# Weighting the experts' rows in their tiles and adding them in DRAM, instead of reading them back and combining them

## The chip, the cores and the metric

The kernel runs on one core of one Trainium2 chip. The metric is the device time of one execution in microseconds. Three timed runs of the kernel before took 3605.23, 3607.03 and 3609.01 us; the median is 3607.03 us.

## The reference, cut to what matters

The program is two layers, each a graph attention network and a feed-forward part, on 4096 rows of 256 floats, with a residual sum after every part. The change lies wholly in the last part, a mixture of six experts with the best two chosen for each row:

```python
def _L1_ffn_ref(features, router_w1, ..., expert_b3):      # E, TOP_K = 6, 2
    rh = relu(features @ router_w1 + router_b1)
    expert_logits = softmax(rh @ router_w2 + router_b2)
    top_w, top_i = top_k(expert_logits, TOP_K)
    routing_weights = softmax(top_w)
    h1 = relu(einsum('bsd,edh->bseh', features, expert_w1) + expert_b1)
    h2 = relu(einsum('bseh,ehf->bsef', h1, expert_w2) + expert_b2)
    expert_out = einsum('bsef,efo->bseo', h2, expert_w3) + expert_b3
    sel = take_along_axis(expert_out, top_i[:, :, :, None], axis=2)
    return sum(sel * routing_weights[..., None], axis=2)

x = x + _L1_ffn_ref(layernorm(x)[None], ...)[0]
```

All of it is in 32-bit floats. The kernel computes an expert only for the rows that chose it.

## The kernel before, in words

The program is written with a framework that sets semaphores by itself and orders the instructions of each engine by its own scheduler, so the order on an engine is not always that of the source. In the source, `P` is 128, `C` is 256, `G` is 4, so a group is 512 rows and there are `NG` = 8 groups; `T` is 2 · 4096 / 256 + 5 = 37 tiles of `TR` = 256 rows.

The first three parts (attention, a feed-forward of 30 steps, two more attention layers) end at about 3240 us of the profiled span. The last part has four stages.

*Router* (L808 to L853). For each group of 512 rows the kernel loads the rows from `x3d` (L92), takes the layer norm on DVE (L100, L833), writes the normed rows `n` to the DRAM tensor `nd` (L836), turns them with PE (L113), copies them to SBUF (`fT`, L838, ACT), and multiplies by the router's weights (L822, L845). The hidden layer `rh` is made by ACT (L824). ACT also writes the rows less 1 to the SBUF tile `acc` (L839), which holds all 4096 rows; the residual stream carries a 1 too much, hence the 1. While this goes on, SP's queue brings in the experts' weights (L857).

*List* (L860 to L1036). DVE picks the two best experts of each row, counts the rows of each expert and lays the 8192 pairs of row and choice into 37 tiles, each tile of one expert. Places that stay empty are padded. The results are `source`, the row that a place reads from `nd`; `dest`, the row of the DRAM tensor `yd` that it writes; and `ws`, the two weights of each row. In `yd` each pair of row and choice has a row of its own: row `n` for the first choice, 4096 + `n` for the second, and rows after that for the padding.

*Tiles* (L1038 to L1146). For each tile, POOL gathers two times 128 rows from `nd` into `gx` (L1048, four buffers); PE turns them (L1060), DVE copies them (`xT`, L1062); PE computes two hidden layers (L1083) and the result (L1104), with weights that DVE and ACT copy for the tile's expert (L1076); ACT (L1094) and DVE (L1096) add bias and take the ReLU. DVE adds the last bias (`ye`, L1112, three buffers) and POOL scatters the 256 rows to `yd`, in two transfers of 128 rows (L1114). The scatters are declared independent of one another:

```python
for before_ in scatters:
    tc.declare_no_dep(ins.ins, before_, reason="a permutation: ...")
scatters.append(ins.ins)
```

In the source, iteration `i` issues the gather of tile `i + 2`, the first hidden layer of tile `i`, the result and scatter of tile `i − 1`, the turning of tile `i + 1` and the second hidden layer of tile `i`.

*End* (L1147 to L1163). After the last scatter SP's queue loads, group by group, both choices' rows from `yd` (16 loads of 512 KB, L1149). DVE multiplies each by its weight and adds it to `acc` (64 operations, L1160), and ACT's queue writes the group to the output (8 writes of 512 KB, L1163).

Of the kernel before, what the change touches and what calls it, by code (L numbers as in the profile page):

```python
# [44 lines left out]
def gnn_ffn_kernel(ctx: ExitStack, tc: tile.TileContext, a: dict, out: bass.AP):  # L45
# [732 lines left out]
    with ExitStack() as scope:  # L778
# [2 lines left out]
        T2 = 2 * T  # L781
        one = scope.enter_context(tc.tile_pool(name="m_one", bufs=1))
        bT = one.tile([P, NB], F32, name="bT")
        acc = one.tile([P, NT, C], F32, name="acc")
        ws = one.tile([P, 2, NT], F32, name="ws")
        bsel = one.tile([P, T, 2 * KC], F32, name="bsel")
        expert = one.tile([P, T], I32, name="expert")
        dest = one.tile([P, T2], I32, name="dest")
        source = one.tile([P, T2], I32, name="source")
        ew = [one.tile([P, E, KC, C], F32, name=f"ew{i}") for i in range(3)]  # L790
        b3 = one.tile([P, E, C], F32, name="b3")
        nd = dram.tile([N, C], F32, name="nd")
        yd = dram.tile([2 * N + T * TR, C], F32, name="yd")

        with ExitStack() as rs:
            work = rs.enter_context(tc.tile_pool(name="r_work", bufs=2))
# [7 lines left out]
            ps = bank("ps_s")  # L804
            nc.tensor.transpose(ps[:, :NB], br, ident[:NB, :NB])
            nc.vector.tensor_copy(bT, ps[:, :NB])

            lg = rone.tile([P, NT, E], F32, name="lg")  # L808
            rows, stds, fTs, rhs = {}, {}, {}, {}
# [2 lines left out]
            for g in range(NG + 2):  # L812
                if 1 <= g and g + 2 < NG and g + 2 not in ahead:
                    load_ahead(x3d, g + 2, runs_of)
                if g < NG:
                    rows[g] = ahead.pop(g)
                    stds[g] = over_std(work, rows[g])
                if 2 <= g:
                    ps = bank("ps_r")
                    fT = fTs.pop(g - 2)  # L820
                    for k in range(KC):
                        nc.tensor.matmul(ps[:RH], rw1[:, k, :], fT[:, k, :], start=(k == 0), stop=(k == KC - 1))  # L822
                    rh = rhs[g - 2] = work.tile([RH, GR], F32, name="rh")
                    nc.scalar.activation(rh, ps[:RH], AF.Relu, bias=bT[:RH, 0:1])  # L824
                if 1 <= g <= NG:
                    u = g - 1
                    t = rows.pop(u)
                    rstd, mv = stds.pop(u)
                    nmr = work.tile([P, G], F32, name="nmr")
                    nc.vector.scalar_tensor_tensor(nmr, mv[:, :, 0], -1.0, rstd, op0=OP.mult, op1=OP.mult)  # L830
                    n = work.tile([P, G, C], F32, name="n")
                    for r in range(G):
                        nc.vector.tensor_scalar(  # L833
                            n[:, r, :], t[:, r, :], rstd[:, r : r + 1], nmr[:, r : r + 1], op0=OP.mult, op1=OP.add
                        )
                    nc.sync.dma_start(runs_of(nd, u), n)  # L836
                    fT = fTs[u] = work.tile([P, KC, GR], F32, name="fT")
                    nc.scalar.copy(fT, transposed(ps_t, n))  # L838
                    nc.scalar.activation(acc[:, u * G : (u + 1) * G, :], t, AF.Identity, bias=mone)  # L839
                if 2 <= g:  # L840
                    u = g - 2
                    rh = rhs.pop(u)
                    ps = bank("ps_l")
                    for r in range(G):
                        nc.tensor.matmul(  # L845
                            ps[:, r * E : (r + 1) * E], rh[:, r * P : (r + 1) * P], rw2, start=True, stop=True
                        )
                    nc.vector.tensor_tensor(
                        lg[:, u * G : (u + 1) * G, :],
                        ps[:, : G * E].rearrange("p (r e) -> p r e", e=E),  # L850
                        rb2[:, None, :].to_broadcast([P, G, E]),
                        OP.add,
                    )  # L853
# [14 lines left out]
            HB = NT // 2  # L868
            along = numbers("along", [(1, max(T, N // TR))], 0, 0)
            along16 = numbers("along16", [(1, P), (0, HB)], 0, 0, F16)  # L870
            place = numbers("place", [(P, T2)], 2 * N + GR, 1)


            code = rone.tile([P, 2, NT, 2], F16, name="code")
# [36 lines left out]
            for i in range(2):  # L911
                tops.append(best(lg, f"top{i}"))
                oh = hot[:, i]
                nc.vector.tensor_tensor(oh, lg, over(tops[i]), OP.is_equal)
                nc.vector.tensor_tensor(oh, oh, order, OP.mult)
                nc.vector.tensor_tensor(oh, oh, over(best(oh, f"at{i}")), OP.is_equal)
                if i == 0:
                    nc.vector.scalar_tensor_tensor(lg, oh, -4.0, lg, op0=OP.mult, op1=OP.add)

# [77 lines left out]
            df = rone.tile([P, T2], F32, name="df")  # L999
            nc.vector.scalar_tensor_tensor(df, lst[:, :, 1], float(GR), lst[:, :, 0], op0=OP.mult, op1=OP.add)  # L1000
            nc.vector.scalar_tensor_tensor(df, df, -float(GR), none, op0=OP.add, op1=OP.add)
            sf = rone.tile([P, T2], F32, name="sf")
            nc.vector.tensor_scalar(sf, df, float(N), -float(N), op0=OP.is_ge, op1=OP.mult)
            nc.vector.tensor_tensor(sf, sf, df, OP.add)
            nc.vector.tensor_scalar(source, sf, float(N - 1), None, op0=OP.min)
            nc.vector.tensor_copy(dest, df)

            seen = rone.tile([P, T, E - 1], F32, name="seen")
            nc.vector.tensor_tensor(
# [17 lines left out]
                OP.mult,  # L1027
            )
            nc.vector.tensor_reduce(bsel, sel, axis=AX.X, op=OP.add)

            w1, w2 = ws[:, 0], ws[:, 1]
            nc.vector.tensor_tensor(w2, tops[1], tops[0], OP.subtract)
            nc.scalar.activation(w2, w2, AF.Exp)
            nc.vector.tensor_scalar(w1, w2, 1.0, None, op0=OP.add)
            nc.vector.reciprocal(w1, w1)
            nc.vector.tensor_tensor(w2, w2, w1, OP.mult)  # L1036

        work = scope.enter_context(tc.tile_pool(name="m_work", bufs=3))  # L1038
        ps_t = scope.enter_context(tc.tile_pool(name="m_pst", bufs=2, space=PSUM))
        ps_h = scope.enter_context(tc.tile_pool(name="m_psh", bufs=2, space=PSUM))  # L1040
        ps_o = scope.enter_context(tc.tile_pool(name="m_pso", bufs=2, space=PSUM))
        rows, xT, hT, which, held = {}, {}, {}, {}, {}
        scatters = []

        def gather(i):
            rows[i] = work.tile([P, 2, C], F32, name="gx", bufs=4)
            for r in range(2):
                nc.gpsimd.indirect_dma_start(  # L1048
                    out=rows[i][:, r, :],
                    out_offset=None,  # L1050
                    in_=nd[:, :],
                    in_offset=bass.IndirectOffsetOnAxis(ap=source[:, 2 * i + r : 2 * i + r + 1], axis=0),
                )

        def turn(i):
            src = rows.pop(i)
            pt = ps_t.tile([P, KC, TR], F32, name="pt")
            for k in range(KC):
                for r in range(2):
                    nc.tensor.transpose(pt[:, k, r * P : (r + 1) * P], src[:, r, k * P : (k + 1) * P], ident)  # L1060
            xT[i] = work.tile([P, KC, TR], F32, name="xT")
            nc.vector.tensor_copy(xT[i], pt)  # L1062

# [34 lines left out]
        def result(i):  # L1098
# [11 lines left out]
                    )  # L1110
            y = work.tile([P, 2, C], F32, name="ye")
            nc.vector.tensor_tensor(y, po, b3[:, bass.DynSlice(which[i], 1)].to_broadcast([P, 2, C]), OP.add)  # L1112
            for r in range(2):
                ins = nc.gpsimd.indirect_dma_start(  # L1114
                    out=yd[:, :],
                    out_offset=bass.IndirectOffsetOnAxis(ap=dest[:, 2 * i + r : 2 * i + r + 1], axis=0),
                    in_=y[:, r, :],
                    in_offset=None,
                )
                for before_ in scatters:  # L1120
                    tc.declare_no_dep(
                        ins.ins, before_, reason="a permutation: no two of the list's places have one row of yd"
                    )
                scatters.append(ins.ins)

        gather(0)
# [1 line left out]
        for i in range(T + 1):  # L1128
# [15 lines left out]
            if i < T:  # L1144
                hidden(i, 1, h)
                last_h = hT.pop(i)  # L1146
        def back(g, i):  # L1147
            y = work.tile([P, G, C], F32, name="y", bufs=8)
            nc.sync.dma_start(y, runs_of(yd, i * NG + g))  # L1149
            return y  # L1150

        ys = {}
        for g in range(NG + 3):
            if g < NG:
                ys[g] = [back(g, i) for i in range(2)]
            if 3 <= g:
                for i, y in enumerate(ys.pop(g - 3)):
                    for r in range(G):
                        t = (g - 3) * G + r
                        nc.vector.scalar_tensor_tensor(  # L1160
                            acc[:, t, :], y[:, r, :], ws[:, i, t : t + 1], acc[:, t, :], op0=OP.mult, op1=OP.add
                        )
                nc.scalar.dma_start(runs_of(out, g - 3), acc[:, (g - 3) * G : (g - 2) * G, :])  # L1163


# [28 lines left out]
```

## Time and profile before

| what | us |
|---|---|
| median of three runs (lowest to highest) | 3607.03 (3605.23 to 3609.01) |
| the profiled execution | 3589.64 |
| its span, from first to last instruction | 3587.7 |
| router stage, about | 3238 to 3292 |
| list, about | 3292 to 3327 |
| tiles, first gather to last scatter's start | 3327.7 to 3548.4 |
| end | 3548.4 to 3587.7 |

The profile is of one execution. Its engines are PE (matrix products), PEld (PE's weight loads), DVE, ACT and POOL; SP only issues transfers. A line of the timeline gives start, duration, engine, line of the kernel, operation and, in brackets, the idle time of the engine before it and what ended that. Releasers are inferred from semaphore events: where the engine named had long been done, it was another one. A table by stretches gives the busy time of each engine in each, the clock granted to PE, the share of time in which the DMA engines were busy, and what they moved in GB/s. A line on a DMA queue gives packets, megabytes, and the share of the 16 DMA engines' time.

The granted clock of the whole execution was 0.963. On POOL, the 74 gathers have a median of 962 ns each and land 2.8 us after their start; the 74 scatters have 986 ns and land after 2.4 us.

### The profile page before, as it was taken

How to read it: one execution, taken by the hardware profiler on the slowest of the kernel's cores; microseconds unless marked ns; L12 is line 12 of the kernel's file. 1: busy time of each engine (PE TensorE's matmuls, PEld its weight loads, DVE VectorE, ACT ScalarE, POOL GpSimd, SP SyncE). 2: the span in 40 equal slices, each digit the busy share in tenths (PEclk: the TensorE clock that was granted, in tenths of full speed). 3: DMA queues.
4: the chain of work that ended last, by engine and by line, in shares of the span. 5: the costliest groups of instructions: out<-in, count | busy, mean ns of one | idle time of the engine just before them, and what ended most of it. 6: DMA issues, size and time to landing. Idle time of an engine off the chain costs nothing. (4 is left out here: it accounts for less than half of the span.)

```text
span 3587.7 us, 81089 instructions
## 1 busy us (share of the span) xinstructions
PE 3264.7 (91%) x33523; PEld 2981.2 (83%) x33523; DVE 3002.9 (84%) x6039; ACT 2615.2 (73%) x2902; POOL 1100.6 (31%) x899
## 2 busy tenths in 40 slices
PE   6889999996999999999998899999979999996895
PEld 5779889885888888888886889888878888884784
DVE  6899999997877777877786899999889999997445
ACT  2688888886766666666663999999789999993221
POOL 3211101005877777777761000000000000001662
PEclk8899999998999999999998999999999999997897
DMA  6897887501000000000015031321212231314224
GB/s 136 145 232 141 192 196 135 168 22 55 1 1 1 1 1 1 1 1 1 1 31 194 17 119 33 125 75 66 85 66 78 89 123 44 119 25 135 83 95 182
DMA packets 280202, 288.48 MB, mean 80 GB/s; under 512 B 97149, under 2 KB 230426, under 8 KB 279834
## 3 DMA queue, kind: packets, MB, share of 16 engines
q1 hardware_dynamic: 198770, 224.18, 19.2%
q0 software_dynamic: 73920, 52.97, 9.7%
q10 hardware_dynamic: 7144, 6.16, 0.6%
q8 instruction: 264, 4.33, 0.5%
q14 instruction: 104, 0.85, 0.1%
HBM read 248.01 MB, written 68.81 MB: 88 GB/s over the span
## 5 line engine op out<-in xcount | busy, mean ns | idle before, releaser
L565 PE MATMUL acc<-vals,m 128*128 128x130 f16 (+1 forms) x24576 | 1726.6, 232 | 128.2 <-DVE u L475 89.0
L565 PEld LDWEIGHTS <-m 128*128 128x128 bf16 x24576 | 1625.2, 98 | 215.6 <-issue 95.5
L464 ACT ACTIVATE st<-f1b,f2b 128x1024 bf16<-128x1024 f32 (+2 forms) x1664 | 1660.2, 1071 | 152.6 <-DVE m L533 144.8
L533 DVE TENSOR_TENSOR m<-st,m 128x2048 bf16<-128x2048 bf16 (+2 forms) x832 | 938.1, 1137 | 37.0 <-PE acc L565 28.4
L708 PE MATMUL po<-wT,zT 128*128 128x256 f32 x3840 | 875.1, 381 | 10.3 <-ACT zT L734 10.1
L708 PEld LDWEIGHTS po<-wT,zT 128*128 128x128 f32 x3840 | 715.8, 192 | 99.8 <-ACT zT L734 12.4
L694 POOL TENSOR_TENSOR th<-th,y 128x1024 f32<-128x1024 f32 x240 | 567.8, 2367 | 196.2 <-ACT th L693 195.4
L538 DVE TENSOR_TENSOR m<-m,m 128x2048 bf16<-128x2048 bf16 (+2 forms) x520 | 592.8, 1140 | 25.1 <-PE tp_m L217 0.5
L105 POOL TENSOR_TENSOR ln_rstd<-ln_rstd,mhalf 128x4 f32<-128x4 f32 x272 | 281.7, 1036 | 904.1 <-DVE ln_rstd L104 877.3
L100 DVE BATCH_NORM_STATS2 ln_st<-z 128x6 f32<-128x256 f32 x960 | 337.9, 413 | 191.3 <-ACT z L699 191.3
L734 ACT COPY zT<-tp 128x1024 f32<-128x1024 f32 x240 | 242.8, 1012 | 323.7 <-PE tp L113 323.7
L718 DVE SCALAR_TENSOR_TENSOR y<-po,ln_rstd,bias 128x256 f32<-128x256 f32 x928 | 378.6, 469 | 5.2 <-PE po L708 4.4
L699 ACT ACTIVATE z<-th 128x1024 f32<-128x1024 f32 x240 | 254.5, 1060 | 18.5 <-POOL th L694 18.2
L113 PE MATMUL tp<-ident,z 128*128 128x128 f32 x1920 | 251.2, 274 | 12.3 <-ACT z L699 12.3
L113 PEld LDWEIGHTS tp<-ident,z 128*128 128x128 f32 x1920 | 225.9, 142 | 38.9 <-ACT z L699 15.3
L693 ACT ACTIVATE th<-y 128x1024 f32<-128x1024 f32 x240 | 251.2, 1047 | 4.8 <-DVE y L718 4.7
L207 POOL DMA_DIRECT2D rows<-in_adj_dram x80 | 72.9, 912 | 490.6 <-PE tp_m L217 490.3
L447 POOL MEMSET hs<- 128x4 f32 x3 | 0.3, 101 | 630.5 <-DVE u L488 609.1
L305 PE MATMUL ph<-g_w,xT 128*128 128x264 f32 x384 | 112.6, 454 | 30.9 <-DVE v L375 27.7
L305 PEld LDWEIGHTS ph<-g_w,xT 128*128 128x128 f32 x384 | 84.5, 227 | 50.8 <-issue 16.6
L1076 ACT COPY w<-ew 128x512 f32 x37 | 22.7, 617 | 132.8 <-PE ph L1083 103.5
L475 DVE TENSOR_TENSOR u<-acc,lo 128x520 f32<-128x520 f32 (+1 forms) x104 | 66.6, 654 | 49.0 <-ACT lo L474 48.8
(209 smaller groups left out, 2141.6 us busy)
## 6 DMA issues: line engine op xcount, KB each, us to landing
m<-edges SPq DMA_DIRECT2D x32, 2048.0 KB
rows<-in_adj_dram POOLq DMA_DIRECT2D x64, 448.0 KB, 8.0
edges<-ms SPq DMA_DIRECT2D x64, 448.0 KB
m<-edges SPq DMA_DIRECT2D x16, 1792.0 KB
f1b<-fd SPq DMA_DIRECT2D x32, 512.0 KB
rows<-x1d SPq DMA_DIRECT2D x16, 512.0 KB
y<-yd SPq DMA_DIRECT2D x16, 512.0 KB
f1b<-fd SPq DMA_DIRECT2D x16, 448.0 KB
```

What stands on the lines that cost most here:

```text
L100: nc.vector.bn_stats(st[:, r, :], src[:, r, :])
L105: nc.gpsimd.tensor_tensor(rstd, rstd, mhalf, OP.pow)
L113: nc.tensor.transpose(ps[:, k, r * P : (r + 1) * P], src[:, r, k * P : (k + 1) * P], ident)
L464: nc.scalar.activation(st[:, s, :w], f1b[c, h][:, :w], AF.Relu, bias=f2b[:, 2 * q + s, h : h + 1], scale=BIG)
L533: nc.vector.tensor_tensor(m1[:, :, :w], st[:, :, :w], m, OP.logical_and if turned(q) else OP.min)
L538: nc.vector.tensor_tensor(m2[:, :, :w], m, m1[:, :, :w], OP.subtract)
L565: nc.tensor.matmul(acc[:, i, cols], lhs[:, s, rows], v[:, cols], start=(j == 0 and n_ == 0), stop=(j == NT - 1 and n_ == 1), skip_group_ch ...
L693: nc.scalar.activation(th[at], y[:, g * G : (g + 1) * G, :], AF.Tanh, scale=0.01)
L694: nc.gpsimd.tensor_tensor(th[at], th[at], y[:, g * G : (g + 1) * G, :], OP.add)
L699: nc.scalar.activation(z, th.pop(at - 1), AF.Silu, scale=0.01)
L708: nc.tensor.matmul(po[:, r, :], src[:, k, r * P : (r + 1) * P], wT[:, k, :], start=(k == 0), stop=(k == KC - 1),)
L718: nc.vector.scalar_tensor_tensor(y[:, g * G + r, :], po[:, r, :], rstd[:, r : r + 1], last if end else bias, op0=OP.mult, op1=OP.add,)
```

## The change

The experts' results are multiplied by their weights inside the tile loop and are added to the residual rows in DRAM.

- In the router stage ACT's residual rows go to a two-buffer tile `x3` and from there to rows 0 to 4095 of `yd`. `yd` shrinks to 4096 + 256 rows; the last 256, for the padding, are filled with zeros.
- `nd` gets two more columns. The weights of both choices are worked out earlier in the list stage and written into these columns, 8 bytes for each row, by eight transfers on SP. The writes of the normed rows become pieces of 1 KB with a step of 1032 bytes.
- `dest` loses the distinction of the choices (4096 is taken away for a second choice), and padding places of all tiles share the same 256 rows. `which2` keeps which of the two choices a place belongs to.
- In a tile, the gather brings 258 columns; DVE picks the weight of the place (`both`, `weight`), ACT multiplies the two halves of the result by it, and the scatter is a transfer that adds to what `yd` holds.
- Only the two scatters of one tile are still declared independent; a scatter now depends on those of the tile before it.
- At the end there are eight copies from `yd` to the output, DRAM to DRAM, in turn on SP's and ACT's queues. `acc`, the loads and the 64 DVE operations are gone.

```diff
-        acc = one.tile([P, NT, C], F32, name="acc")
-        ws = one.tile([P, 2, NT], F32, name="ws")
+        which2 = one.tile([P, 2, T2], F32, name="which2")
-        nd = dram.tile([N, C], F32, name="nd")
-        yd = dram.tile([2 * N + T * TR, C], F32, name="yd")
+        nd = dram.tile([N, C + 2], F32, name="nd")
+        yd = dram.tile([N + TR, C], F32, name="yd")
...
+            nothing = rone.tile([P, 2, C], F32, name="nothing")
+            nc.gpsimd.memset(nothing, 0.0)
+            nc.sync.dma_start(yd[N:, :].rearrange("(p r) c -> p r c", r=2), nothing)
...
-                    nc.sync.dma_start(runs_of(nd, u), n)
+                    nc.sync.dma_start(runs_of(nd, u)[:, :, :C], n)
...
-                    nc.scalar.activation(acc[:, u * G : (u + 1) * G, :], t, AF.Identity, bias=mone)
+                    x3 = work.tile([P, G, C], F32, name="x3")
+                    nc.scalar.activation(x3, t, AF.Identity, bias=mone)
+                    nc.sync.dma_start(runs_of(yd, u), x3)
...
-            place = numbers("place", [(P, T2)], 2 * N + GR, 1)
+            place = numbers("place", [(0, T), (P, 2)], 2 * N + GR, 1)
...
+            ws = rone.tile([P, NT, 2], F32, name="ws")
+            w1, w2 = ws[:, :, 0], ws[:, :, 1]
+            nc.vector.tensor_tensor(w2, tops[1], tops[0], OP.subtract)
+            nc.scalar.activation(w2, w2, AF.Exp)
+            nc.vector.tensor_scalar(w1, w2, 1.0, None, op0=OP.add)
+            nc.vector.reciprocal(w1, w1)
+            nc.vector.tensor_tensor(w2, w2, w1, OP.mult)
+            for g in range(NG):
+                nc.sync.dma_start(runs_of(nd, g)[:, :, C:], ws[:, g * G : (g + 1) * G, :])
...
-            sf = rone.tile([P, T2], F32, name="sf")
-            nc.vector.tensor_scalar(sf, df, float(N), -float(N), op0=OP.is_ge, op1=OP.mult)
-            nc.vector.tensor_tensor(sf, sf, df, OP.add)
-            nc.vector.tensor_scalar(source, sf, float(N - 1), None, op0=OP.min)
+            nc.vector.tensor_scalar(which2[:, 1], df, float(N), None, op0=OP.is_ge)
+            nc.vector.scalar_tensor_tensor(df, which2[:, 1], -float(N), df, op0=OP.mult, op1=OP.add)
+            nc.vector.tensor_scalar(source, df, float(N - 1), None, op0=OP.min)
             nc.vector.tensor_copy(dest, df)
+            nc.vector.tensor_scalar(which2[:, 0], which2[:, 1], -1.0, 1.0, op0=OP.mult, op1=OP.add)
...
-        scatters = []
...
-            rows[i] = work.tile([P, 2, C], F32, name="gx", bufs=4)
+            rows[i] = work.tile([P, 2, C + 2], F32, name="gx", bufs=4)
...
+            both = work.tile([P, 2, 2], F32, name="both")
+            nc.vector.tensor_tensor(
+                both, src[:, :, C:].rearrange("p r s -> p s r"), which2[:, :, 2 * i : 2 * i + 2], OP.mult
+            )
+            weight[i] = work.tile([P, 2], F32, name="weight", bufs=4)
+            nc.vector.tensor_tensor(weight[i], both[:, 0], both[:, 1], OP.add)
...
+            w = weight.pop(i)
+            scatters = []
             for r in range(2):
+                nc.scalar.activation(y[:, r, :], y[:, r, :], AF.Copy, scale=w[:, r : r + 1])
                 ins = nc.gpsimd.indirect_dma_start(
                     out=yd[:, :],
                     out_offset=bass.IndirectOffsetOnAxis(ap=dest[:, 2 * i + r : 2 * i + r + 1], axis=0),
                     in_=y[:, r, :],
                     in_offset=None,
+                    compute_op=OP.add,
                 )
                 for before_ in scatters:
-                    tc.declare_no_dep(ins.ins, before_, reason="a permutation: ...")
+                    tc.declare_no_dep(ins.ins, before_, reason="no row is twice among an expert's")
                 scatters.append(ins.ins)
...
-        (back: 16 loads of yd, 64 weighted additions to acc, 8 writes to the output)
+        for g in range(NG):
+            (nc.sync, nc.scalar)[g % 2].dma_start(runs_of(out, g), runs_of(yd, g))
```

## The prediction

> **What bounds the kernel now.** The chain of waits puts the end of the program in the mixture-of-experts part; everything up to about 3240 us is attention and feed-forward code that the diff does not touch. So I cut the last 350 us into stages first (busy time of each engine by stretch):
>
> ```profile
> core 0: us, PE busy (x) PEld busy (x) DVE busy (x) ACT busy (x) POOL busy (x), PEclk, DMA share, GB/s
> 3238.00:3292.00 54.00, 41.63 (x223) 27.18 (x221) 32.47 (x132) 23.41 (x27) 15.89 (x30) 0.84 0.64 213
> 3292.00:3327.00 35.00, 9.55 (x68) 8.49 (x68) 30.70 (x64) 0.69 (x3) 0.00 (x0) 0.56 0.05 18
> 3346.00:3518.00 172.00, 172.00 (x857) 151.85 (x857) 83.51 (x154) 44.75 (x92) 120.75 (x123) 1.00 0.30 94
> 3549.00:3588.00 39.00, 0.00 (x0) 0.00 (x0) 26.22 (x64) 0.00 (x0) 0.34 (x1) 0.50 0.84 326
> ```
>
> Four stages with four limits: the router (PE and latency), the list making (DVE, DMA idle at 0.05), the loop over 37 tiles (PE busy 172.00 of 172.00), and a tail of 39 us in which DMA runs at 0.84 and PE not at all. Next, one period of the loop in the timeline, POOL and then PE's weight loads:
>
> ```profile
> 3402.03 0.96 POOL L1048 DMA_INDIRECT gx<-nd,source  x1 [0.77 <-PE pt L1060]
> 3403.30 1.00 POOL L1114 DMA_INDIRECT yd<-ye,dest  x1 [0.30 <-issue]
> 3404.60 0.99 POOL L1114 DMA_INDIRECT yd<-ye,dest  x1 [0.30 <-issue]
> 3405.89 0.99 POOL L1048 DMA_INDIRECT gx<-nd,source  x1 [0.30 <-issue]
> 3407.65 0.96 POOL L1048 DMA_INDIRECT gx<-nd,source  x1 [0.77 <-PE pt L1060]
> ```
> ```profile
> 3403.11 1.70 PEld L1083 LDWEIGHTS ph<-xT,w 128*128 128x128 f32 x8
> 3404.83 1.70 PEld L1104 LDWEIGHTS po<-ew,h 128*128 128x128 f32 x8
> 3406.56 0.57 PEld L1060 LDWEIGHTS pt<-ident,gx 128*128 128x128 f32 x4
> 3407.10 1.60 PEld L1083 LDWEIGHTS ph<-h,w 128*128 128x128 f32 x8
> ```
>
> The period is 3407.65 − 3402.03 = 5.62 us. PE's loads abut: 1.70 + 1.70 + 0.57 + 1.60 = 5.57, so **PE sets the pace**. POOL is second: four transfers of 0.96 to 1.00 plus three gaps of 0.30 and one of 0.77. Only the 0.77 exceeds the usual 0.30, so POOL has 0.47 us of slack per tile. One answer of the waits misleads:
>
> ```profile
> DVE ye L1112 <- DMA yd<-ye,dest: 33.7, 29, 1.2
> ```
>
> It says results wait for scatters. But the ye at 3401.35 is the eleventh (first 3345.16, 5.62 apart) and its buffer, one of three, was scattered at 3386 to 3388, landing by 3391. It was released by PE; the scatter of 3398.98 only happens to land then (2.4 us later). No scatter holds the loop. Last, the tail:
>
> ```profile
> 3548.38 0.97 POOL L1114 DMA_INDIRECT yd<-ye,dest  x1 [0.30 <-issue]
> 3550.92 21.91 SPq L1149 DMA_DIRECT2D y<-yd  x16
> 3557.83 26.38 ACTq L1163 DMA_DIRECT2D out_dram<-acc  x8
> q1 hardware_dynamic: 2304, 8.39, 61.2%
> q10 hardware_dynamic: 1152, 4.19, 28.5%
> ```
>
> From the last scatter's start to the end of the span are 3587.7 − 3548.4 = 39.3 us. In them 8.39 MB come back and 4.19 MB go out, at 350 GB/s: bound by DMA.
>
> **What the Trainium skill says.** All from "DMA: Bandwidth & Descriptors". "Rules for kernel authors": an accumulating transfer reads its destination and writes it later, so an earlier one to the same bytes must be waited for by its semaphore; no run here shows it, since before there is no such transfer. "Two DMAs through the same engine are not ordered": two read-modify-writes issued back to back overlap, the second reading before the first has written; I conclude that the rows of one transfer are pipelined. "Latency and other measured facts": copies from HBM to HBM reached 207 to 214 GB/s in each direction. The trace has no such copy; with one side in SBUF it shows 350 GB/s. The price of an accumulation stands on no page.
>
> **Part by part.** *Tail.* Removed: 16 loads and 64 DVE operations of L1160. Added: 8 copies of 512 KB on SP and ACT, 4.19 MB. At 214 GB/s (the skill's figure, my estimate) that is 19.6 us. Two bounds: 4.19 MB at the 381 GB/s that q1 shows (8.39 MB in 61.2% of 36 us) is 11 us; at 175, if the 4 KB pieces cost more, 24. Around it: landing of the last scatter 3.5 (below), 0.1 to issue, 1.0 to first bytes (SP issues at 3550.92, DMA is busy from about 3551.9), 1.0 for the last receipt (2.4 landing − 0.97 issue − 0.41 transfer). Sum 25.2; gain 39.3 − 25.2 = 14.1, ends 9 and 23.
>
> *Loop, compute.* DVE gets two 128x4 and 128x2 operations per tile, about 0.15 each (nmr L830 is 0.152); ACT gets two scalings of 128x256, 0.84 together (as the pair of L1094). DVE is at 84 of 172 us, ACT at 45: both stay hidden behind PE. The gather now also waits for the DVE product that reads its last two columns; ye ends at 3402.04, the product at about 3402.2, so the gather starts 0.3 to 0.4 later. Queued behind it are the two scatters and the next gather; all slide by the same 0.4 once, since POOL's 5.13 still fits in 5.62. Gathers run six tiles ahead of the scatters in POOL's order (14 before the first scatter), so PE does not see it. Rows of 1032 instead of 1024 B: hidden, DMA share is 0.30. At the last tile nothing covers the scaling: +0.5.
>
> *Loop, the new wait.* A scatter of tile i may start only when both of tile i−1 have landed. Behind the waiting instruction stand a scatter and two gathers; PE would wait for those gathers. The loop through POOL is: start of the first to start of the second scatter 1.30, landing L, waking 0.30. It binds if 1.30 + L + 0.30 > 5.62, that is **L > 4.0**. A plain scatter lands in 2.4, a gather in 2.8. An adding one reads HBM like a gather and writes HBM like a scatter: at most their sum less the shared 0.97 of issue, 4.2; at least 2.4. I take 3.5: hidden by the two gathers issued between. This is only an estimate: the adder itself could cost more.
>
> *POOL's issue cost.* An adding descriptor has two sources. L207 issues 448 KB, 896 rows, in 0.91 us, as long as 128 indirect rows, so rows are not what POOL pays for. I take 1.05; ends 0.97 and 1.5. Slack 0.47 over two scatters: it binds from 1.22.
>
> *Router.* acc (L839) becomes a two-buffer tile with a write of 512 KB per group: 4.19 MB, plus 0.26 MB of zeros, are added to the 11.5 MB of 54 us (213 GB/s), making 295 GB/s, below the 350 seen. Row loads queued behind on SP come up to 8 us ahead of use (issued 3254.12, used 3262 and later). L839, 1.15 us, no longer runs early (four of them by 3252) but within each group's 4.35 us; in the worst order it stands ahead of rh: 1.15 × 6 = 7. I take +2.0, ends 0 and 8. The weights: 4096 pieces of 8 B in nd, behind the expert weights on the rings. 256 B pieces took 17.7 ns each (2080 in 6.4% of 16 × 36 us); at that price 4.5 us over 16 engines, at four times that 18. They are known at 3298.6 and the first gather starts at 3327.7: cover 29 us, at nothing; if the expert weights end 15 us later that cover is gone, and the 8 above includes it. Moved weight formulas sit among the top-two operations already in the trace (3297.2 to 3298.6): nothing. The list gets as many DVE operations before source as before: nothing.
>
> **Sum:** −14.1 + 0.5 + 2.0 = −11.6. The profiled execution took 3589.64 us (span 3587.7 and 1.9 around it), so 3578.0 there; the runs' median is 17.4 higher, 3607.0, and the same difference gives **3595.4**.
>
> **Rivals.** *A, the additions pace the loop* (slower). L = 5 makes the period 1.30 + 5 + 0.30 = 6.60, 0.98 more in 36 steps = +35; with −11.6 that is +24, 3631. It eats the gain from L = 4.3 and is measurably slower from L = 4.5. For it: nothing here prices the adder. Against: the 4.2 bound, and pipelined rows. POOL paying 1.5 per issue (+0.55 × 37 = +20) would look alike but leave no waits.
>
> *B, no change.* The copy at 175 GB/s (gain 9), and the router at +5: −4, 3603. For it: router groups are tight and SP carries 17 more transfers; against: DMA idles at 0.05 after.
>
> *C, the copy runs at the rate of plain transfers:* gain 23 − 2.5 = 20, 3587. In the name of the change nothing else is promised that could fail to be done.
>
> **How the numbers follow.** Expected case, C included, 0.58; A 0.27; B 0.15. About 0.2% (7 us) can be told from no change. Expected: 0.52 faster, 0.06 within. A: 0.25 slower, 0.02 within. B: 0.02 faster, 0.09 within, 0.04 slower. Together 0.54, 0.17, 0.29. The range reaches from C (3586) to A at L = 5 (3631), leaving out some 0.05 below and 0.13 above.
>
> **What would show it.** Right: tile period still 5.62, PE loads abutting, adding scatters landing in under 4.0 us, POOL's operation about 1.05; a tail of about 25 us with no DVE; first gather near 3330. Wrong: POOL idle before scatters released by a scatter's landing, PE waiting for gathered rows; POOL's scatter above 1.22; the list stage waiting for SP; or a copy under 175 GB/s.

## The result, and the profile after

The kernel became slightly slower. Its median is 3616.1 us (3613.2 to 3619.1), beside 3606.1 us for the kernel before (3598.7 to 3609.0), a ratio of 1.0036 with a 95% interval of [1.0019, 1.0052]: 7 to 19 us more. The prediction said 3595.4. The profiled execution of after took 3619.08 us (span 3617.3). The table by stretches shows where to look (columns: stretch, its length, busy time of PE, PE's loads, DVE, ACT and POOL with their instructions, granted PE clock, DMA share, GB/s):

```profile
core 0: us, PE busy (x) PEld busy (x) DVE busy (x) ACT busy (x) POOL busy (x), PEclk, DMA share, GB/s
3346.00:3518.00 172.00, 153.53 (x733) 128.34 (x732) 70.67 (x181) 59.57 (x130) 132.43 (x103) 0.99 0.50 80
3518.00:3597.00 79.00, 63.46 (x290) 53.32 (x289) 28.93 (x67) 23.93 (x52) 50.50 (x37) 0.92 0.46 61
3597.00:3618.00 21.00, 0.00 (x0) 0.00 (x0) 0.00 (x0) 0.00 (x0) 1.30 (x1) 0.50 0.71 212
```

In the same stretch of 172 us in which PE was busy all the time before, it is now busy for 153.53, in the 79 us behind it for 63.46. The last row is the copy: 21 us without DVE, where before there were 39. So the tail gave more than was hoped for and the tile loop took back more than that. One period of the loop, POOL alone in the timeline:

```profile
3384.97 1.63 POOL L1131 DMA_INDIRECT yd<-ye,dest  x1 [0.30 <-ACT h L1108]
3386.90 1.59 POOL L1131 DMA_INDIRECT yd<-ye,dest  x1 [0.30 <-issue]
3388.79 1.02 POOL L1056 DMA_INDIRECT gx<-nd,source  x1 [0.30 <-issue]
3390.12 0.98 POOL L1056 DMA_INDIRECT gx<-nd,source  x1 [0.30 <-issue]
3391.47 1.62 POOL L1131 DMA_INDIRECT yd<-ye,dest  x1 [0.36 <-issue]
```

The gaps are 0.30 almost throughout, the usual space between two of POOL's transfers: POOL has no slack left. The gathers cost what they did; an adding scatter takes 1.6 us instead of 0.99. The period is 3391.47 − 3384.97 = 6.50 us, against 5.62 before. The waits of the last part name two more things:

```profile
DVE both L1070 <- DMA gx<-nd,source: 105.7, 37, 5.2
ACT ye L1130 <- DVE ye L1126: 93.8, 32, 4.7
PEld ph L1097 <- DVE xT L1076: 31.1, 24, 2.7
```

(Total us, times, longest.) DVE stands for 105.7 us before its new product with the gathered weights, and PE's loads wait 31.1 us for turned rows. And at the end of the loop, once the gathers are done, the scatters stand in pairs with 2.9 us ahead of each pair:

```profile
3582.21 1.55 POOL L1131 DMA_INDIRECT yd<-ye,dest  x1 [2.94 <-ACT h L1108]
3584.07 1.55 POOL L1131 DMA_INDIRECT yd<-ye,dest  x1 [0.31 <-issue]
3588.59 1.55 POOL L1131 DMA_INDIRECT yd<-ye,dest  x1 [2.96 <-DMA yd<-ye,dest]
3590.44 1.55 POOL L1131 DMA_INDIRECT yd<-ye,dest  x1 [0.30 <-issue]
3594.89 1.55 POOL L1131 DMA_INDIRECT yd<-ye,dest  x1 [2.89 <-issue]
3596.74 1.55 POOL L1131 DMA_INDIRECT yd<-ye,dest  x1 [0.30 <-issue]
3600.40 2.81 SPq L1164 DMA_DIRECT2D out_dram<-yd  x4
3600.41 2.52 ACTq L1164 DMA_DIRECT2D out_dram<-yd  x4
```

Only one pair has its cause printed (a landing of `yd`), but the steps are regular: 3582.21, 3588.59, 3594.89, that is 6.4 and 6.3 us. So three causes are in question: what POOL pays for an adding transfer, the wait of a tile's additions for those of the tile before, and DVE's new order.

### The profile page after: what moved, and what is told of

It reads as the page before. It is cut to its first block, busy times and chain, and to the rows that moved or that the text cites. A ratio compares the mean times of both kernels' runs of the same rounds, so it can differ in the third digit from the quotient of the medians.

```text
span 3617.3 us, 81156 instructions
## 1 busy us (share of the span) xinstructions
PE 3278.2 (91%) x33523; PEld 2982.0 (82%) x33523; DVE 2980.9 (82%) x6050; ACT 2648.9 (73%) x2976; POOL 1150.7 (32%) x900
## 3 DMA queue, kind: packets, MB, share of 16 engines
q0 software_dynamic: 81024, 53.04, 11.3%
## 5 line engine op out<-in xcount | busy, mean ns | idle before, releaser
L699 ACT ACTIVATE z<-th 128x1024 f32<-128x1024 f32 x240 | 254.7, 1061 | 16.9 <-POOL th L694 16.5
L305 PE MATMUL ph<-g_w,xT 128*128 128x264 f32 x384 | 123.8, 488 | 31.3 <-DVE v L375 27.7
L305 PEld LDWEIGHTS ph<-g_w,xT 128*128 128x128 f32 x384 | 91.9, 247 | 55.1 <-issue 16.6
L1131 POOL DMA_INDIRECT yd<-ye,dest x74 | 118.2, 1597 | 42.3 <-issue 22.3
```

What stands on the lines that cost most here:

```text
L699: nc.scalar.activation(z, th.pop(at - 1), AF.Silu, scale=0.01)
```

## The experiments

Total times scatter between runs of one kernel, by up to 22 us for the kernel before (3591.5 to 3613.9 in one group of runs), so the table cuts each profiled execution into stages: *tiles* from the first gather to the last scatter's start, *of it last* from the last gather on, *tail* from the last scatter's start to the end of the span. Scatter is the median duration of POOL's instruction. Each ratio, with its 95% interval, is to runs of the kernel before that stood beside the kernel's own; their medians lay between 3598.6 and 3606.1 us, so the times of two rows are not to be subtracted.

| kernel | tiles, us | of it last | tail, us | scatter, us | time, us | ratio to before |
|---|---|---|---|---|---|---|
| before, first profile | 220.7 | 30.1 | 39.3 | 0.99 | 3589.6 | |
| before_again | 230.6 | 29.9 | 38.5 | 1.00 | 3601.9 | |
| after | 261.1 | 41.5 | 20.6 | 1.59 | 3616.1 | 1.0036 [1.0019, 1.0052] |
| after_again | 260.5 | 41.2 | 20.3 | 1.59 | 3613.9 | |
| adds_alone | 237.8 | 21.8 | 41.0 | 1.59 | 3638.7 | 1.0113 [1.0094, 1.0131] |
| copy_alone | 230.7 | 30.7 | 18.8 | 1.00 | 3584.1 | 0.9961 [0.9947, 0.9975] |
| no_add | 235.5 | 35.0 | 18.8 | 0.99 | 3585.7 | 0.9968 [0.9959, 0.9977] |
| two_targets | 253.6 | 35.7 | 20.3 | 1.59 | 3605.1 | 1.0021 [1.0012, 1.0029] |
| late_both | 257.0 | 35.1 | 20.5 | 1.58 | 3607.6 | 1.0031 [1.0018, 1.0044] |
| late_two | 239.1 | 21.9 | 19.9 | 1.58 | 3591.7 | 0.9979 [0.9970, 0.9988] |
| late_two_sp | 217.8 | 34.0 | 20.4 | 1.55 | 3568.5 | 0.9916 [0.9899, 0.9932] |
| half_rows | 242.3 | 36.4 | 19.2 | 1.41 | 3586.6 | |
| half_cols | 255.9 | 38.3 | 21.4 | 1.59 | 3609.5 | |
| half_back | 231.9 | 30.6 | 34.5 | 1.00 | 3595.8 | 0.9992 [0.9983, 1.0001] |
| half_in_tile | 248.3 | 29.2 | 29.4 | 0.99 | 3612.7 | 1.0025 [1.0016, 1.0033] |

Kernels without a ratio have one time only, that of the profiled execution.

**The kernel before once more.** It is unaltered, so that its stages can be compared with those of the first profile.

> The kernel before, unaltered, profiled once more, to see how far one execution differs from another in code that nothing touches. Expected: tiles period 5.62 us and end of 39 us as in the first profile; if its span is again near 3588 us the timed runs carry something that the profile lacks, if it is near 3605 us the first profile was a lucky one, and the stages show where.

Its time was 3601.9 us, 12 more than the first profile, and 10 of these are in the tiles: 230.6 instead of 220.7. Its timeline shows where PE loses its pace there:

```profile
3442.76 0.50 DVE L1076 COPY w<-ew 128x512 f32 x1 [1.45 <-PE ph L1083]
...
3444.94 0.69 DVE L1112 TENSOR_TENSOR ye<-po,b 128x512 f32<-128x512 f32 x1 [1.68 <-PE pt L1060]
3445.55 0.68 DVE L1062 COPY xT<-pt 128x512 f32<-128x512 f32 x1
3446.29 1.59 PEld L1083 LDWEIGHTS ph<-xT,w 128*128 128x128 f32 x8 [0.68 <-DVE xT L1062]
```

In every second tile DVE's `ye` comes late, the copy of the turned rows stands behind it, and PE's loads wait for it, here 0.68 us. The kernel before thus has two paces of its tile loop; copy_alone (230.7) and half_back (231.9), whose loops are also without the additions, show the slower one too. Some 10 of the 17 us between the first profile and the median are likely this, though only profiled executions show it. What brings on one pace or the other was not settled. After took 261.1 and 260.5 us in its two profiles. It is compared with 230.6, the pace of three profiles out of four.

**Only the adding.** Before, with additions in place of plain writes; `yd` is filled with zeros early.

```diff
+        for k in range(yd.shape[0] // (6 * P)):      # 23 transfers, during the feed-forward part
+            nc.sync.dma_start(yd[k * 6 * P : (k + 1) * 6 * P, :]..., zeros.to_broadcast([P, 6, C]))
...
                     in_offset=None,
+                    compute_op=OP.add,
```

> The kernel before with one thing added: its scatters add, to a target that was filled with zeros during the feed-forward steps; every row is still hit once, so no scatter waits for another, and weights, copies and end are those of before. Theory 1 (POOL pays 1.6 us instead of 1.0 to issue an adding scatter, and is then the slowest engine): POOL's period is 2 x 1.60 + 2 x 0.98 + 4 x 0.30 = 6.4 us, the tiles stage grows by about 28 us and the time by about 25 to 30. Theory 2 (the wait of one tile's additions for the last tile's sets the pace): period 5.62, time as before within 5 us. Theory 3 (the scaling and the product that waits for the gather hold DVE and ACT): as theory 2.

```profile
3440.58 1.62 POOL L1120 DMA_INDIRECT yd<-ye,dest  x1 [0.30 <-DVE w L1082]
3442.50 1.58 POOL L1120 DMA_INDIRECT yd<-ye,dest  x1 [0.30 <-issue]
3444.38 1.02 POOL L1054 DMA_INDIRECT gx<-nd,source  x1 [0.30 <-issue]
3445.70 0.98 POOL L1054 DMA_INDIRECT gx<-nd,source  x1 [0.30 <-PE ph L1089]
3446.98 1.62 POOL L1120 DMA_INDIRECT yd<-ye,dest  x1 [0.30 <-issue]
```

All scatters are still independent here, there is no scaling, and DVE's order is the old one. Even so each addition takes 1.6 us, all gaps are 0.30, and POOL's period is 6.40. The stage of 237.8 is POOL's issue from end to end: 20.6 us from the first gather to the first scatter, then the other gathers (about 60) at 1.30 and 74 scatters at 1.9 make 239. It is 17 us more than in the first profile and 7 more than in before_again; the expectation of 28 overlooked that POOL is freed of gathers at the end, where the last part fell to 21.8. Of the 40 us by which the whole is slower, some 27 lie ahead of the router, in the feed-forward part where the zeros were written; they say nothing on what the scatters cost, and the ratio is not used.

**Only not the adding.** After, with `compute_op=OP.add` taken out.

> The kernel after with plain scatters in place of adding ones; the wait of each tile's scatters for the last tile's stays, as do weights, scaling, nd's rows and the copy at the end (the sum over the two choices and the residual is left out). Theories 1 and 2: scatters issue in 1.0 and land in 2.4 us, period 5.62, tiles stage about 222 us, time 38 to 40 us below after, that is 20 to 28 below before. Theory 3: period stays near 6.5 us and the time at that of after.

```profile
L1131 POOL DMA_INDIRECT yd<-ye,dest x74: 965/986/1016, 3353.2 to 3564.5; - x74
```

(Tile view: lowest, median and highest ns, first and last start.) The same instruction at the same place costs 0.99 again and the stage falls from 261.1 to 235.5. Everything else that the change put into the tiles (wider gathers, scaling, weights, the wait for earlier writes) costs 5 us beside the 230.6. With the adding in it, the kernel is slower than before, and without it faster, by 0.3% and not by the 20 to 28 us expected, which were reckoned from a stage of 222. The run takes away two things at once, the dearer issue and whatever later landing an addition has; the next ones tell more.

**Only the copy.** Before, with its end replaced.

```diff
-        (16 loads of yd, 64 weighted additions to acc, 8 writes to the output)
+        for g in range(NG):
+            (nc.sync, nc.scalar)[g % 2].dma_start(runs_of(out, g), runs_of(yd, g))
```

> The kernel before with only its end changed: eight copies of yd's first 4096 rows to the output instead of the 16 loads, 64 sums and 8 writes (the sum over choices and the residual is left out). It measures the gain of the end by itself: from the last scatter to the end 39.3 us before, 20.6 in after; expected 19 to 20 us here (a plain scatter lands 1 us sooner), so 19 to 20 below before.

The tail is 18.8 instead of 38.5, with the tiles unchanged (230.7 beside 230.6): some 20 us. The ratio of the whole gives 9 to 19.

**The wait for the tile before.** After, with tiles in turn added to one of two tensors; the second one's sums are left out of the output. A scatter then has until two tiles later.

```diff
-                    out=yd[:, :],
+                    out=(yd, yd2)[i % 2][:, :],
```

> The kernel after with the additions of odd tiles going to a second tensor of the same size, so that a scatter waits for the tile before the last one, twice as long ago (the odd tiles' share of the sum is left out; a copy of one tensor at the end as in after). Theory 1: POOL's four transfers still need 6.4 us, so the period stays at 6.4 and only the last five tiles, where no gathers stand between, get faster: 3 to 5 us below after. Theory 2: the wait is gone, period 5.62, 30 to 35 us below after. Theory 3: as after.

The stage fell by 7.5 us, from 261.1 to 253.6, of which 5.8 are in the last part, where no gathers stand between the scatters. POOL's period while it gathers hardly changed:

```profile
3444.40 1.63 POOL L1132 DMA_INDIRECT yd<-ye,dest  x1 [0.30 <-issue]
...
3450.84 1.63 POOL L1132 DMA_INDIRECT yd<-ye,dest  x1 [0.30 <-issue]
```

6.44 us. The wait is real, but it is not what paces the loop while there are gathers to issue.

**DVE's order.** In after, the scheduler put the product `both` of a tile three tiles ahead of the copy `xT` of the same tile. There it waits for POOL's newest gather, with the work of earlier tiles behind it:

```profile
3420.14 0.16 DVE L1070 TENSOR_TENSOR both<-gx,which 128x4 f32<-128x4 f32 x1 [3.86 <-DMA gx<-nd,source]
3420.64 0.43 DVE L1090 COPY w<-ew 128x512 f32 x1 [0.34 <-issue]
3420.99 0.68 DVE L1126 TENSOR_TENSOR ye<-po,b 128x512 f32<-128x512 f32 x1
3421.59 0.68 DVE L1076 COPY xT<-pt 128x512 f32<-128x512 f32 x1
3422.32 1.59 PEld L1097 LDWEIGHTS ph<-xT,w 128*128 128x128 f32 x8 [1.88 <-DVE xT L1076]
```

DVE stands 3.86 us for an operation of 0.16; then `ye` and `xT` run at once, and PE, which had waited for `xT` for 1.88 us, goes on. The experiment keeps everything and emits the copy first, with a fixed order behind it on DVE:

```diff
+            turned_ = nc.vector.tensor_copy(xT[i], pt)          # was behind weight[i]
             both = work.tile([P, 2, 2], F32, name="both")
-            nc.vector.tensor_tensor(
+            ins = nc.vector.tensor_tensor(both, ...)
+            tc.add_manual_dep(ins.ins, turned_.ins.name, <order only, no semaphore>, ...)
```

> The kernel after with one order changed: on DVE the product both is issued behind the copy xT of its own tile, instead of three tiles ahead of it, where it waits for a gather that is not needed yet and holds ye and xT of earlier tiles behind it. Theory 4 (besides POOL's dearer issue, this wait ties PE to the newest gather, so PE cannot run ahead of POOL and the last six tiles are left to do after the last gather): the tiles stage shrinks from 261 to about 247 us, DVE's 106 us of waits for gathers go, and the time falls 10 to 15 below after, to about that of before. Rival (POOL's issue and the wait for the last additions are all): within 3 us of after.

Alone it gives 4.1 us of the stage (257.0), not the 14 expected; the ratio, 1.0031 [1.0018, 1.0044], cannot be told from that of after.

**Both at once.**

> Both product late and additions of odd tiles to a second tensor (their share of the sum left out): what remains is POOL's issue alone. By it: 23 us to the first scatter, then 60 gathers of 1.31 and 74 scatters of 1.90 us, 219 us, a tiles stage of 242 us against 261 in after; time about 19 us below after, 8 below before. If the stage is still above 250, something else is in it.

```profile
3443.68 1.63 POOL L1138 DMA_INDIRECT yd<-ye,dest  x1 [0.30 <-issue]
3445.61 1.58 POOL L1138 DMA_INDIRECT yd<-ye,dest  x1 [0.30 <-DVE h L1117]
3447.49 1.02 POOL L1057 DMA_INDIRECT gx<-nd,source  x1 [0.30 <-issue]
3448.82 0.98 POOL L1057 DMA_INDIRECT gx<-nd,source  x1 [0.30 <-issue]
3450.11 1.61 POOL L1138 DMA_INDIRECT yd<-ye,dest  x1 [0.30 <-issue]
```

The two edits gave 4.1 and 7.5 us alone; together they give 22.0 (261.1 to 239.1). Each hid the other, and the last part shows how. In after, the scatters of seven tiles follow the last gather, 6.3 us apart, the pace of the wait ("of it last", 41.5 us). Without the wait (two_targets) they are seven, 5.62 apart, PE's pace: 35.7. Without the tie of PE to the newest gather (late_both) they are six, still some 6.3 apart: 35.1. Without both they are six, 3.72 apart:

```profile
3566.11 1.55 POOL L1138 DMA_INDIRECT yd<-ye,dest  x1 [0.30 <-ACT ye L1137]
3567.97 1.55 POOL L1138 DMA_INDIRECT yd<-ye,dest  x1 [0.30 <-issue]
3569.83 1.55 POOL L1138 DMA_INDIRECT yd<-ye,dest  x1 [0.30 <-ACT ye L1137]
```

That is POOL's two additions alone (21.9 us), since PE has some of these tiles behind it: DVE has started 33 of the 37 `ye` before the last gather, 31 in after. What remains is POOL: 239.1 against 237.8 in adds_alone, the same pattern of 0.30 gaps and a period of 6.43.

The other part of the stage, up to the last gather, is "tiles" less "of it last". It is 216 to 222 us in the six kernels that issue whole adding scatters between gathers (after, after_again, adds_alone, two_targets, late_both, late_two) and 200 to 201 in before_again, copy_alone and no_add (190.6 in the first profile). So POOL's dearer issue costs 15 to 22 us there, whatever becomes of the wait and the order; these two are paid for behind the last gather. And with the dearer issue alone the change would still have paid: late_two's scatters take 1.58 us, and its ratio is 0.9979 [0.9970, 0.9988], a little below before, though its output still lacks the second tensor's sums.

**And without the gathers on POOL.** late_two, with the rows brought by SP from fixed places instead of gathered, so that the right rows are left out.

```diff
-                nc.gpsimd.indirect_dma_start(out=rows[i][:, r, :], ..., in_=nd[:, :], in_offset=...)
+                at = (2 * i + r) % NT * P
+                nc.sync.dma_start(rows[i][:, r, :], nd[at : at + P, :])
```

> As late_two, with the gathers replaced by plain loads of 128 rows on SP (fixed rows of nd, so neither the rows nor the sum are those wanted): POOL has only two additions of 1.90 us per tile, 3.8 us. If POOL's issue is the bound, PE takes over at 5.62 us per tile, the stage is about 225 us and the time 35 to 40 below after. If the adding transfers themselves (DMA engines, HBM) are the bound, the period stays above 6.

```profile
core 0: us, PE busy (x) PEld busy (x) DVE busy (x) ACT busy (x) POOL busy (x), PEclk, DMA share, GB/s
3346.00:3500.00 154.00, 154.00 (x768) 135.65 (x767) 78.23 (x192) 65.37 (x137) 86.33 (x56) 1.00 0.60 96
```

```profile
L1134 POOL DMA_INDIRECT yd<-ye,dest x72: 1537/1551/1569, 3351.1 to 3548.3; - x72
...
DMA to landing us min/median/max: 3.6/3.8/5.1
```

PE is busy 154.00 of 154.00 us again and the stage is 217.8. All additions are still made, with a DMA share of 0.60. So what held the loop of late_two at 239.1 was neither the DMA engines nor the DRAM that takes the additions, but POOL's issue. In after, POOL's issue has the same pace up to the last gather, and the wait follows. The second fence also gives the landing: an addition is complete 3.8 us after its start (median).

**What POOL pays for.** After with half the rows in each scatter, and with half the columns (and a `yd` of half the width); the other halves are left out.

```diff
-   out_offset=...(ap=dest[:, ...]), in_=y[:, r, :]
+   out_offset=...(ap=dest[: P // 2, ...]), in_=y[: P // 2, r, :]      # half_rows
+   out_offset=...(ap=dest[:, ...]), in_=y[:, r, : C // 2]             # half_cols
```

> The kernel after with adding scatters of only the first 64 of each 128 rows (the other rows' share is left out). Asks what POOL pays the extra 0.6 us for. If for rows[...], the operation falls by about 0.3 us to 1.3 or lower; if it is a fixed extra of adding, it stays near 1.6 less what half the rows of a plain scatter would save.

> The kernel after with additions of only 128 of the 256 columns, to a target half as wide (the other columns are left out, the end copies the half twice). If POOL pays for rows, its operation stays at 1.6 us; if for bytes, it falls to about 1.3.

```profile
L1131 POOL DMA_INDIRECT yd<-ye,dest x74: 1396/1411/1592, 3347.9 to 3565.7; - x74
```
```profile
L1131 POOL DMA_INDIRECT yd<-ye,dest x74: 1552/1587/1656, 3354.4 to 3586.3; - x74
```

First fence half_rows, second half_cols. Half the bytes leave POOL's time as it was. Half the rows save 0.18 us, 2.8 ns a row. If the time goes evenly with the rows (an estimate from these two points), no rows at all would leave 1.23 us, 0.24 above the whole plain scatter of 128 rows. So at least 0.24 of the extra 0.60 would be a fixed cost of the adding form. How much of the rest is fixed is not shown, since no plain scatter with fewer rows was run. What POOL does in the extra time the profile does not show.

**Two attempts at something better.** Since the copy helps and the additions do not, what is left of the change without adding? half_back is before with `yd`, `ye` and the loaded rows in 16 bits, so that half the bytes come back.

```diff
-        yd = dram.tile([2 * N + T * TR, C], F32, name="yd")
+        yd = dram.tile([2 * N + T * TR, C], F16, name="yd")
...
-            y = work.tile([P, 2, C], F32, name="ye")
+            y = work.tile([P, 2, C], F16, name="ye")
```

> The kernel before with the experts' results scattered and read back as 16-bit floats (yd, ye and y in F16; sums still in 32 bits). Since the end is bound by DMA (12.6 MB in 36 us), reading 4.2 MB instead of 8.4 leaves 8.4 MB, 24 us at the same rate; the loop is unchanged. Expected: end 27 to 29 us, time 10 to 12 us below before. Rival: the 64 operations of DVE at 0.48 us, 31 us, now set the end: gain 5 or less.

```profile
3565.41 15.88 SPq L1149 DMA_DIRECT2D y<-yd  x16
3568.18 25.43 DVE L1160 SCALAR_TENSOR_TENSOR acc<-y,ws,acc 128x256 f32<-128x256 f16 x64 [6.71 <-DMA y<-yd]
3571.47 22.50 ACTq L1163 DMA_DIRECT2D out_dram<-acc  x8
```

The tail shrank by 4 us only, not by the 10 to 12 expected: with fewer bytes, DVE's 64 operations still take 25 us, and the writes follow them. half_in_tile takes those away too: after's weighting in the tile (with the late `both`) and scatters that write 16-bit rows of their own place, so that the end has 16 plain additions instead of 64 weighted ones.

> A version drawn from the runs: weights gathered with the rows and applied in the tile (product behind xT, as in late_both), but plain scatters of 16-bit results to a row per pair, as before, and at the end 16 loads of 256 KB and 16 sums of 128x1024 instead of 64 of 128x256. POOL issues in 1.0 us, no scatter waits for another, and the end is no longer bound by DVE (16 x 1.15 = 18 us) but by 8.4 MB of DMA. Expected: stage as in before (221 to 231), end 27 to 29 us, router 2 us longer, time 7 to 10 us below before. Rival (16-bit sums on DVE or the loads' latency hold the end at 34 as in half_back): 2 us below.

```profile
POOL yd L1132 <- ACT yh L1131: 63.8, 25, 5.4
```

The tail came to 29.4, 9 less than in before_again, but the tiles to 248.3, 18 more: POOL's scatters waited 63.8 us for ACT's scaled halves, on the path from PE's result to the scatter, and the gathers stood behind them. The stage up to the last gather, 219.1, is as long as with additions, but here POOL stands waiting in it. That this wait is the cause of the 18 us was not tested. Neither version beats the kernel before: half_back cannot be told from it, half_in_tile is slower (1.0025).

**After once more**, unaltered.

> The kernel after, unaltered, profiled once more: whether its tiles stage of 261 us is typical, as that of before was found to take 221 in one profile and 231 in two others. If POOL's issue and the two waits account for it, it is 255 to 262 again with the period at 6.4 to 6.6.

260.5 and 20.3, as in the first profile.

## Why the prediction was wrong, step by step

**The first step that failed is "POOL's issue cost".** It took 1.05 us with an upper end of 1.5; measured is 1.59 in after and in adds_alone, outside the bounds. The argument was that rows are not what POOL pays for. half_rows bears this out in part (2.8 ns a row, some 0.35 us of 1.59), but the argument says nothing on a fixed cost of the adding form, and by the estimate above there is one. The rest of the step was sound: with 1.59 in place of 1.05, POOL's period is 2 × 1.59 + 1.02 + 0.98 + 4 × 0.30 = 6.4 us, as measured in adds_alone, 0.8 above PE's 5.62. In after this costs 19 us up to the last gather (219.6 beside 200.7).

**"Loop, the new wait" failed too: it was mis-sized.** The sum was 1.30 + 3.5 + 0.30 = 5.1, below 5.62 and so hidden. Measured is 6.3: start to start of the two scatters 1.85 (1.30 plus the dearer issue), and 4.45 from the second's start to the next tile's first. Of that, 3.8 is landing, as seen in late_two_sp (the estimate of 3.5 was near), and about 0.65 waking, twice the figure taken. With the predicted issue it would still be 1.35 + 4.45 = 5.8, by estimate, just above PE's pace. The 6.3 lies under POOL's 6.4, so the wait shows only once the gathers are gone. There the Trainium skill's rule ("DMA: Bandwidth & Descriptors", section "Rules for kernel authors"), which asks an addition to wait for an earlier one to the same bytes, has a price in these runs; that the wait is needed no run tested. The conclusion drawn from "Two DMAs through the same engine are not ordered", that rows of one transfer overlap, fits a landing 1.4 us above a plain scatter's 2.4, but no run tested it either.

**"Loop, compute" missed the order on DVE, which it put at nothing.** `both` was costed at 0.15 us and the gather that waits for it was followed, but not what stands behind `both` on DVE when the gather is late. Not the duration but the place of an instruction of 0.16 us made 105.7 us of DVE's waits. What it costs depends on the rest: 4.1 us where the wait for the last tile stays, 14.5 where that is gone (two_targets to late_two).

**The tail was right in mechanism and pessimistic in size**: 25.2 predicted, 20.6 measured. Up to the copy's first issue it was nearly exact (3.6 predicted, 3.7 measured). The copy with its start and receipt was put at 21.6 and took 3617.3 − 3600.4 = 16.9 us for 4.19 MB: 248 GB/s. The skill's "Latency and other measured facts" has 207 to 214 in each direction for copies within HBM, for tiles with rows of 16 KiB; for this copy the measurement decides. The gain was 18 to 19 us, not 14.1. **The router's** +2.0 was measured as +1.6 to +2.7, list included. The eight writes of weights did not show: they were issued from 3305.6 to 3313.0, and the first gather, at 3335.6, was released by DVE's `dest`.

**The sum.** From 230.6 to 260.8 (mean of two) in the tiles is +30, the tail −18, the router +2: +14, and the ratio gives +13. The prediction's was +0.5 − 14.1 + 2.0. Of the +30, 19 lie before the last gather (POOL's issue) and 12 behind it (the wait and the order). With the issue cost alone the last part would have become 8 us shorter instead, as in adds_alone and late_two, and the change would have gained a little. So the issue cost took most of the gain, and only together with the wait and DVE's order did it turn the sign. Against the first profile it would be +40 in the tiles: that profile had the faster of before's two paces, and the prediction carried its difference over to the median as if the loop always ran so.

**The rivals.** A, the additions pace the loop, is what happened, though not by the landing alone, on which its sum rested, and for the greater part in the form that the prediction gave one sentence: "POOL paying 1.5 per issue (+0.55 × 37 = +20) would look alike but leave no waits". C was near with the gain of the copy (20), though the copy did not run at the 381 GB/s of plain transfers. A step whose point of decision, 1.22, lay in the middle of its own bounds, 0.97 to 1.5, was given as if settled.

## What to carry to other kernels

Where a change puts a new form of instruction on the engine that comes second by a small margin (here 0.47 us of 5.62), the form's issue cost decides which engine sets the pace, and an argument from the nearest known form does not bound it: let the chance follow from how much of the bounds lies on each side of the point of decision. A tiny instruction that waits for a late producer has to be costed by what stands behind it on its engine, in the order in which the scheduler puts it. And where two waits end at nearly the same time, take both away in one experiment: alone they gave 4 and 7.5 us, together 22.

## What the runs showed of the hardware

- An indirect transfer that adds occupies POOL for 1.59 us per 128 rows of 1 KB, a plain one for 0.99. At 64 rows it is 1.41, at half the row's length still 1.59.
- It makes one packet for every row, where a plain scatter makes 32 for 128 rows. The queue of POOL's transfers has 81024 packets in after (first line) and 73920 in no_add (second), 96 fewer for each of 74 scatters; half_rows has 76288, 64 fewer than after for each. The DMA share of the loop was 0.30 at 94 GB/s in before and 0.50 at 80 GB/s in after.

```profile
q0 software_dynamic: 81024, 53.04, 11.3%
q0 software_dynamic: 73920, 53.04, 9.7%
```

- It lands 3.8 us after its start in late_two_sp (plain, in before: 2.4), and in after an addition that depends on it starts 4.45 us after that start.
- A copy from DRAM to DRAM in eight transfers on two queues ran at 248 GB/s, start and receipt included.
